# Mixture-of-experts tail on one core: the last tiles of the experts packed in halves of 64 rows, and the end of the routing rebuilt

## The chip, the cores and the metric

The kernel runs on one core of a Trainium2 chip. The metric is the device time of one execution in microseconds (us). The core has TensorE (PE in the profile; its weight loads are shown as PEld), VectorE (DVE), ScalarE (ACT), GpSimd (POOL) and SyncE (SP), each with its own instruction stream, and 16 DMA engines that all transfers share. "SPq" or "POOLq" is the sequencer of such an engine, which issues transfers and waits on semaphores. In this kernel SP issues the plain loads, and POOL issues the indirect transfers (gathers and scatters by a list of row numbers).

## The reference

The input is 4096 nodes of 512 f32 values and a dense 4096 x 4096 0/1 adjacency matrix. The program computes a masked attention with 8 heads and then a mixture of 8 experts, of which each node uses two:

```python
adj = jnp.maximum(adjacency_matrix, eye)
scores = jnp.einsum('hqk,hmk->hqm', q, k) * kd ** (-0.5)
scores = scores + IDENTITY_BIAS * eye - MASK_VAL * (1.0 - adj)
x = x + einsum('hqm,hmk,hko->qo', softmax(scores), v, Wo)      # q, k, v from layernorm(x)

logits = xf @ Wg + bg                                          # xf = layernorm(x), 8 experts
topk_scores, topk_idx = jax.lax.top_k(logits, 2)
topk_w = jax.nn.softmax(topk_scores, axis=-1)
h = gelu(einsum('nd,edh->neh', xf, W1) + b1)
y = einsum('neh,ehf->nef', h, W2) + b2
out = x + sum over the two chosen experts of topk_w * y
```

Two experts for each of 4096 nodes make 8192 rows of expert work. With the reference's inputs the eight experts get 1087, 1067, 1033, 901, 1076, 1067, 1008 and 953 rows.

## The kernel before, in words

All arithmetic is in f32, and a product of two f32 tiles is issued to TensorE as two instructions. The program has four stages.

**Projections and lists (to about 490 us).** Queries, keys and values are computed and put in DRAM, and for each tile of 128 queries a list of the keys that any of them sees is built.

**Attention (to about 1500 us).** It goes over 32 query tiles and, within each, over tiles of 128 listed keys; `items` is the list of these (query tile, key tile) pairs. POOL gathers the keys of an item `AHEAD=9` items ahead. The order of all instructions is written out by hand (`tc.manual_schedule()`): an item `n` issues the turning of keys for `n+3`, the scores of `n+2` and the value product of `n`, and between them come the jobs of `route(g)`. There, a group of finished query tiles (`GROUPS`: seven groups of four tiles, then 2, 1 and 1) is normalized, its gate logits are computed (`pg`, `pl`, `l`), the two best experts are found (`rank`, `chosen`), each row gets a place in its expert's region of `xs_d` (`place`, `slot`, `slot_i`), the running `count` per expert is raised, and the rows are scattered to `xs_d` by POOL (L825), one scatter for each query tile and each of the two choices. The scatters wait in the list `waiting`. They are issued when a group two later begins, or all at once after the last item. `slot_i` (L808, L809) has two buffers, so the third group in a row waits until the scatters of the first have read theirs.

**The end of the routing.** After the last item SP loads the second layer's weights `w2` (L1215, eight loads of 1 MB), and VectorE checks whether any sum of the attention left its safe bounds (`bad`, L1227 to L1237). The result goes to a register of every engine (L1241), and a branch skips a fallback body (L1244). Then `finish_routing` (L836 to L893) makes from `count` a table with one entry per expert tile (which expert, from which row), with operations that are 71 tiles x 8 experts wide (L860 to L877), and the marks `first` and `mine`. A tile is 128 rows of one expert's region; the last tile of an expert is laid so that it ends at the region's end, so it may overlap the one before it, and `mine` sends the overlapping rows to a spare place.

**Expert tiles (`work_off`, L1357 to L1454).** 69 tiles run (`MOSTLY`); two more stand in a branch on the register `more`, which is 0 for these inputs. For tile b:

- `fetch(b)`, four tiles ahead: SP reads expert and start row from the table (L1368, L1372) and loads 128 rows `r` (L1377, five buffers) and both biases spread over 128 partitions (`bb`, L1379 and L1380, four buffers).
- `turn` transposes the rows on TensorE (`pt_e`, L209) and ScalarE copies them (`xT`).
- `hidden` multiplies by W1 (`ph`, L1391: four f32 products of 512 columns, 8 instructions), VectorE adds b1 (L1396), ScalarE applies gelu (L1397).
- `turn_hidden` transposes that (`pht`, L1403), VectorE copies it to `hT` (L1405).
- `second` computes the gate (L1411, L1414), multiplies by W2 (`py`, L1420, 8 instructions), VectorE adds b2 (`y`, L1425, three buffers), ScalarE scales by the gate (L1426), VectorE makes the target rows `to` (L1429, L1433, eight buffers), and POOL scatters y onto the output with an add (L1434).

The scatter-adds all write the output, so each waits for the landing of the one before it:

```python
nc.gpsimd.indirect_dma_start(
    out=out,
    out_offset=bass.IndirectOffsetOnAxis(ap=to[:, 1:2].bitcast(I32), axis=0),
    in_=y, in_offset=None, compute_op=ALU.add,
)
```

In this stage a scheduler places the instructions on each engine; an engine runs its own in that order, so one that waits holds all behind it. PE's order for a tile is `pht(b)`, `ph(b+1)`, `pt_e(b+2)`, `py(b)`.

Of the kernel before, what the change touches and what calls it, by code (L numbers as in the profile page):

```python
# [20 lines left out]
P = 128  # L21
# [22 lines left out]
def kernel(  # L44
# [30 lines left out]

    nc = tc.nc
# [15 lines left out]
    NB = (2 * N + E * (P - 1)) // P  # L92
    MOSTLY = NB - 2
# [74 lines left out]
    first = const.tile([P, NB], F32, name="first")  # L168
    table = const.tile([1, 2 * NB], I32, name="table")
    mine = const.tile([P, NB], F32, name="mine")  # L170
# [621 lines left out]
    def route_3(m, l, rank, pp, rows, pool, name):  # L792
# [15 lines left out]
        slot_i = pool.tile([P, m, 2], I32, tag="slot_i", name=f"slot_i_{name}")  # L808
# [27 lines left out]
    def finish_routing(pool, psum):  # L836

        pn = psum.tile([P, E], F32, name="pn")
        nc.tensor.matmul(pn, ones, count, start=True, stop=True)
        many = pool.tile([P, E], F32, name="many")  # L840
        nc.vector.tensor_copy(many, pn)
        more = pool.tile([P, E, NT], F32, name="more")
        nc.vector.tensor_tensor(
            more, many.unsqueeze(2).to_broadcast([P, E, NT]),
            full.unsqueeze(1).to_broadcast([P, E, NT]), op=ALU.is_gt,
        )
        tiles_e = pool.tile([P, E], F32, name="tiles_e")
        nc.vector.tensor_reduce(tiles_e, more, axis=AX.X, op=ALU.add)
        none = pool.tile([P, E], F32, name="none")
        nc.vector.memset(none, 0.0)  # L850
        upto = pool.tile([P, E], F32, name="upto_e")
        nc.vector.tensor_tensor_scan(
            upto, tiles_e, none, initial=0.0, op0=ALU.add, op1=ALU.add
        )
        nc.vector.tensor_scalar(
            none[:1, :1], upto[:1, E - 1 : E], -float(MOSTLY), 0.0, op0=ALU.add, op1=ALU.max
        )
        nc.vector.tensor_copy(beyond, none[:1, :1])
        past = pool.tile([P, NB, E], F32, name="past_e")
        nc.vector.tensor_tensor(  # L860
            past, nth.unsqueeze(2).to_broadcast([P, NB, E]),
            upto.unsqueeze(1).to_broadcast([P, NB, E]), op=ALU.is_ge,
        )

        end = pool.tile([P, E + 1], F32, name="end")
        nc.vector.memset(end[:, E:], float(E * R + P))
        nc.vector.tensor_add(end[:, :E], many, start_e)
        more_e = pool.tile([P, E], F32, name="more_e")
# [33 lines left out]
    with tc.tile_pool(name="p2a", bufs=2) as two, tc.tile_pool(  # L902
# [274 lines left out]
        for n, (i, c) in enumerate(items):  # L1177
            begin()
            if n + AHEAD < len(items):
                fetch(n + AHEAD)  # L1180
            if c == 2 and i + 1 < NT:
                load_q(i + 1)
# [35 lines left out]
        while n <= len(items) + LAST or jobs or first_of_step:  # L1218
            begin()
            later(n)  # L1220
            while waiting:
                waiting.pop(0)[1]()
# [282 lines left out]
```

## Time and profile before

| | |
|---|---|
| runs | 2105.8, 2101.3, 2100.26 us (median 2101.3) |
| the profiled execution | 2098.63 us, of which its span 2096.9 us, so 1.73 us outside the span |
| mean granted TensorE clock | 0.984 |
| busy share of the span | PE 96%, PEld 64%, DVE 62%, POOL 49%, ACT 45% |
| attention's last TensorE work | about 1502 us |
| first `r` load issued | 1543.60 us |
| first `py` | 1561.21 us |
| last scatter-add begins on POOL | 2090.57 us |

The page of a profile gives the busy time of each engine, the same in 40 slices of the span, the DMA queues, the chain of waits that ended last, and the costliest groups of instructions. A line such as "1525.82 0.17 DVE L809 CAST ... [11.21 <-DMA xs_d<-rows,slot_i]" of a timeline reads: start at 1525.82 us, 0.17 us long, on VectorE, from line 809, after VectorE had been idle for 11.21 us, which a DMA that writes `xs_d` and reads `rows` and `slot_i` ended.

### The profile page before, as it was taken

To read this page: it belongs to the slowest core of one execution; us is meant where nothing else is said; L and a number is where in the kernel's file an instruction comes from. 1 tells how busy PE (TensorE), PEld (TensorE's weight loads), DVE (VectorE), ACT (ScalarE), POOL (GpSimd) and SP (SyncE) were. 2 spreads that over 40 slices of the span, in tenths; PEclk is the share of its full clock that TensorE was granted. 3 is DMA by queue.
4 is the path that set the end of the run, shared out by engine and by line. 5 is a ranking of instruction groups with operands and counts; after the bars stand their busy time and mean duration, and the time that the engine had idled before them with its cause. 6 is when DMAs were issued, how large, how long until landed. Compare 5 with 4: busy or idle time off the path is not lost. (4 is left out here: it accounts for less than half of the span.)

```text
span 2096.9 us, 48528 instructions
## 1 busy us (share of the span) xinstructions
PE 2003.1 (96%) x18748; PEld 1331.8 (64%) x18748; DVE 1290.2 (62%) x2446; ACT 941.1 (45%) x1703; POOL 1032.2 (49%) x1067
## 2 busy tenths in 40 slices
PE   8998899999999999999999999999849999999998
PEld 3444444488888788788878778777624444444443
DVE  5786778287767777777777777676733333333332
ACT  3644454365556555556556555555412222222221
POOL 1044445678776676676666657678312211222122
PEclk9999999999999999999999999999969999999999
DMA  8978898778888788788888878777666566656653
GB/s 326 369 277 291 303 316 278 213 239 257 259 272 250 244 279 255 239 276 255 269 266 249 262 213 271 231 235 239 214 186 135 135 136 139 137 133 137 137 140 77
DMA packets 213088, 479.03 MB, mean 228 GB/s; under 512 B 48963, under 2 KB 80963, under 8 KB 208757
## 3 DMA queue, kind: packets, MB, share of 16 engines
q0 software_dynamic: 78944, 241.65, 39.3%
q1 hardware_dynamic: 133380, 233.15, 36.1%
q8 instruction: 153, 2.51, 0.5%
q10 hardware_dynamic: 528, 1.05, 0.2%
q14 instruction: 83, 0.67, 0.1%
HBM read 398.85 MB, written 76.90 MB: 227 GB/s over the span
## 5 line engine op out<-in xcount | busy, mean ns | idle before, releaser
L231 POOL DMA_INDIRECT kv<-kv_d,key_of x363 | 426.0, 1174 | 241.4 <-PE po L1024 156.6
L1012 DVE TENSOR_TENSOR e<-e,mask 128x512 f32<-128x512 f32 (+1 forms) x363 | 322.8, 890 | 202.2 <-ACT e L1004 140.1
L957 ACT COPY kT<-pk 128x512 f32<-128x512 f32 x395 | 232.0, 587 | 279.5 <-PE pk L954 270.1
L1434 POOL DMA_INDIRECT out_dram<-y,to x69 | 107.7, 1561 | 450.0 <-ACT y L1426 439.2
L1030 DVE TENSOR_TENSOR acc<-acc,e 128x512 f32<-128x512 f32 (+1 forms) x363 | 321.4, 885 | 0.0
L1024 PE MATMUL po<-e,kv 128*64 128x64 f32 (+1 forms) x5808 | 303.6, 247 | 0.0
L231 POOL DMA_INDIRECT mask<-in_adjT_dram,mask_of x234 | 263.2, 1125 | 71.3 <-issue 54.2
L1024 PEld LDWEIGHTS po<-e,kv 128*64 128x64 f32 x5808 | 239.6, 137 | 43.8 <-DVE mv L198 0.2
L1001 PE MATMUL s<-q,kT 128*128 128x128 f32 x1832 | 265.1, 288 | 1.5 <-ACT acc L994 1.5
L1391 PE MATMUL ph<-w,xT 128*128 x552 | 250.6, 597 | 0.7 <-ACT xT L210 0.7
L1420 PE MATMUL py<-w,hT 128*128 x552 | 248.5, 593 | 2.0 <-DVE hT L1405 2.0
L1001 PEld LDWEIGHTS s<-q,kT 128*128 128x128 f32 x1832 | 221.6, 191 | 17.0 <-ACT acc L994 1.6
L1004 ACT ACTIVATE e<-s 128x512 f32<-128x512 f32 x229 | 137.1, 599 | 93.2 <-PE s L1001 90.9
L954 PE MATMUL pk<-ident,kv 64*128 64x64 f32 x2904 | 167.7, 235 | 11.7 <-ACT kT L957 10.9
L954 PEld LDWEIGHTS pk<-ident,kv 64*128 64x128 f32 x2904 | 118.1, 138 | 76.5 <-issue 45.9
L231 POOL DMA_INDIRECT pm<-in_adjT_dram,mask_of x129 | 125.9, 976 | 79.4 <-DMA packed_h<-pm 33.4
L1420 PEld LDWEIGHTS py<-w,hT 128*128 128x128 f32 x552 | 99.6, 190 | 102.5 <-issue 99.5
L1391 PEld LDWEIGHTS ph<-w,xT 128*128 128x128 f32 x552 | 100.2, 192 | 100.9 <-issue 99.8
L994 ACT ACTIVATE e<-s 128x512 f32<-128x512 f32 x268 | 145.6, 596 | 38.1 <-PE s L989 37.2
L989 PE MATMUL s<-q,kT 64*128 64x128 f32 x2144 | 148.8, 279 | 0.0
L373 DVE TENSOR_REDUCE flags<-adjT 128x64 f32<-128x4096 f32 x32 | 140.6, 4405 | 11.8 <-DMA adjT<-in_adjT_dram 11.8
L1426 ACT ACTIVATE y<-y,gate 128x512 f32<-128x512 f32 x69 | 49.8, 722 | 212.0 <-DVE y L1425 207.6
(611 smaller groups left out, 2582.7 us busy)
## 6 DMA issues: line engine op xcount, KB each, us to landing
adjT<-in_adjT_dram SPq DMA_DIRECT2D x32, 2048.0 KB
bb<-in_L_ffn_b_dram SPq DMA_DIRECT2D x138, 256.0 KB
r<-xs_d SPq DMA_DIRECT2D x69, 258.0 KB
kv_d<-kv SPq DMA_DIRECT2D x32, 512.0 KB
xt<-in_x_dram SPq DMA_DIRECT2D x32, 256.0 KB
qT_d<-qT SPq DMA_DIRECT2D x8, 1024.0 KB
q<-qT_d SPq DMA_DIRECT2D x64, 128.0 KB
xr<-in_x_dram SPq DMA_DIRECT2D x32, 256.0 KB
```

What stands on the lines that cost most here:

```text
L231: nc.gpsimd.indirect_dma_start(out=to, out_offset=None, in_=src, in_offset=bass.IndirectOffsetOnAxis(ap=of[:, at[i] + c : at[i] + c + 1], ...
L373: nc.vector.tensor_reduce(flags[g][:, :, j, :], adj_in.pop(i).rearrange("p c (h q) -> p h c q", h=2), axis=AX.X, op=ALU.max,)
L954: nc.tensor.transpose(pk[:, r, ts(p, KD)], kv[n][half, ts(p, P)], ident[half, half])
L957: nc.scalar.copy(kT[n].rearrange("k p (r j) -> k r p j", r=2), pk[:, :, : NP * KD].rearrange("k r (p j) -> k r p j", p=NP),)
L989: nc.tensor.matmul(s[r][:, p, :], k[rows, p, :], q_in[i][rows, p, r, :], start=True, stop=True,)
L994: nc.scalar.activation(e.rearrange("p (a r) q -> p r a q", r=2)[:, r], s[r], AF.Exp)
L1001: nc.tensor.matmul(s[:, p], k[:, p, :], q_in[i][:, p, :, q], start=True, stop=True)
L1012: nc.vector.tensor_mul(e, e, m.unsqueeze(1).to_broadcast(e.shape))
L1024: nc.tensor.matmul(po[i][r * KD : (r + 1) * KD, p, q], v[:, ts(h, KD)], e[:, h, :], start=(c < 0 and p == 0), stop=(c == listed[i] - 1), s ...
L1030: nc.vector.tensor_add(acc[i][:, :, q], acc[i][:, :, q], e)
L1391: nc.tensor.matmul(ph, xTs[b][:, c, :], w1[:, bass.ds(es[b], 1), c, :], start=(c == 0), stop=(c == DC - 1),)
L1420: nc.tensor.matmul(py, hTs[b][:, c, :], w2[:, bass.ds(es[b], 1), c, :], start=(c == 0), stop=(c == HC - 1),)
```

## The change

The expert stage now has `NF` = 57 tiles of 128 rows of one expert, as before, and then tiles of two halves of 64 rows. 57 is the least number of full tiles that any split of 8192 rows can have. What is left of the experts is cut in pieces of 64 rows: 14 whole ones at most, and per expert one last piece of under 64 rows. Tiles 57 to 64 hold one whole piece (partitions 0 to 63) and the last piece of expert h = b - 57 (partitions 64 to 127). Tile 65 holds a whole piece alone in 64 rows. So 66 tiles run; five more single pieces stand in the branch on `more`, which is 0 for these inputs too (61 full tiles of 128 can be cut from the counts, of which 57 are used, and nine whole pieces of 64 are left).

In a tile of two halves `product` issues, for each of the four chunks, one f32 product of 64 columns of the array for each half, each with its own expert's weights, so 16 instructions instead of 8 for `ph` and for `py`. `fetch` issues six loads of 64 rows instead of three of 128. `second` issues two scatter-adds: one of the first 64 rows, then one of all 128 rows in which the foreign rows (all of half 0, and what `mine` marks in half 1) are sent to the spare place. The list of targets of the second one, `to2`, has four buffers. In whole tiles `to` is now one copy.

`finish_routing` is rebuilt: it works with operations of 2 x 8 elements and puts the table together by a product with a diagonal (`all_ones`, `diag`, `pt`); it moves ahead of the check's register and branch, and a second copy of it stands in the fallback body. `slot_i` has four buffers. In the last nine items of the attention, which gather nothing any more, each step issues one waiting scatter behind a small memset. The check of the bounds moves to four steps after the last item.

```diff
-    NB = (2 * N + E * (P - 1)) // P
-    MOSTLY = NB - 2
+    HR = P // 2
+    NF = (2 * N - E * (P - 1) + P - 1) // P
+    NH = 2 * N // HR - 2 * NF
+    MOSTLY = E + 1
+    assert NH >= MOSTLY and NH <= P and NF <= P
...
+    first = const.tile([P, NF + NH], F32, name="first")
+    table = const.tile([1, 2 * (NF + NH) + E], I32, name="table")
+    mine = const.tile([P, E], F32, name="mine")
+    row_of = const.tile([P, 2], F32, name="row_of")
...
-        slot_i = pool.tile([P, m, 2], I32, tag="slot_i", name=f"slot_i_{name}")
+        slot_i = pool.tile([P, m, 2], I32, tag="slot_i", bufs=4, name=f"slot_i_{name}")
         nc.vector.tensor_copy(slot_i, slot)
...
-    def finish_routing(pool, psum):
+    def finish_routing(all_ones, pool, psum, tag, name):
+        def column(what, *width):
+            return pool.tile([P, *(width or (1,))], F32, name=f"{what}_{name}")
+        none = column("none", E)
+        nc.vector.memset(none, 0.0)
...
+        pn = psum.tile([P, E], F32, tag=tag, name=f"pn_{name}")
         nc.tensor.matmul(pn, ones, count, start=True, stop=True)
+        ints = pool.tile([P, E], I32, name=f"ints_{name}")
+        nc.vector.tensor_copy(ints, pn)
+        nc.vector.tensor_single_scalar(ints, ints, 7, op=ALU.arith_shift_right)
+        nc.vector.tensor_copy(tiles[:, 0], ints)
         nc.vector.tensor_tensor_scan(
+            upto[:, 0], tiles[:, 0], none, initial=0.0, op0=ALU.add, op1=ALU.add
+        )
+        nc.vector.tensor_sub(used[:, :E], upto[:, 0], tiles[:, 0])
         nc.vector.tensor_scalar(
+            used[:, :E], used[:, :E], -1.0, float(NF), op0=ALU.mult, op1=ALU.add
+        )
+        nc.vector.scalar_tensor_tensor(
+            used[:, :E], used[:, :E], 0.0, tiles[:, 0], op0=ALU.max, op1=ALU.min
+        )
+        rest = column("rest", E)
+        nc.vector.scalar_tensor_tensor(
+            rest, used[:, :E], -float(P), pn, op0=ALU.mult, op1=ALU.add
+        )
+        nc.vector.tensor_copy(ints, rest)
+        nc.vector.tensor_single_scalar(ints, ints, 6, op=ALU.arith_shift_right)
+        nc.vector.tensor_copy(tiles[:, 1], ints)
+        nc.vector.tensor_tensor_scan(
+            upto[:, 1], tiles[:, 1], none, initial=0.0, op0=ALU.add, op1=ALU.add
+        )
+        nc.vector.tensor_scalar(
+            per_e[:, 0], tiles[:, 0], -float(P), float(R), op0=ALU.mult, op1=ALU.add
+        )
+        nc.vector.tensor_sub(per_e[:, 1], used[:, 1:], used[:, :E])
+        nc.vector.scalar_tensor_tensor(
+            per_e[:, 1], per_e[:, 1], 2.0, tiles[:, 1], op0=ALU.mult, op1=ALU.subtract
+        )
+        nc.vector.tensor_scalar(
+            per_e[:, 1], per_e[:, 1], float(HR), float(R), op0=ALU.mult, op1=ALU.add
+        )
+        past = column("past", 2, E)
+        nc.vector.tensor_scalar(past, upto, number, None, op0=ALU.is_le)
+        nc.vector.tensor_mul(per_e, per_e, past)
+        of = column("of", 2, 2)
+        sums = column("sums", 2)
+        nc.vector.tensor_reduce(sums, per_e, axis=AX.X, op=ALU.add)
+        nc.vector.tensor_reduce(of[:, :, 0], past, axis=AX.X, op=ALU.add)
+        nc.vector.tensor_scalar_min(of[:, :, 0], of[:, :, 0], float(E - 1))
+        nc.vector.tensor_add(of[:, :, 1], sums, row_of)
...
+        diag = column("diag", 2 * (NF + NH))
+        for k, (at_k, n) in enumerate(((0, NF), (2 * NF, NH))):
+            nc.vector.tensor_mul(
+                diag[:, at_k : at_k + 2 * n].rearrange("p (j b) -> p j b", j=2),
+                ident[:, :n].unsqueeze(1).to_broadcast([P, 2, n]),
+                of[:, k].unsqueeze(2).to_broadcast([P, 2, n]),
+            )
+        pt = psum.tile([P, 2 * (NF + NH)], F32, tag=tag, name=f"pt_{name}")
+        nc.tensor.matmul(pt, all_ones, diag, start=True, stop=True)
+        nc.vector.tensor_add(end, pn, start_e)
+        nc.vector.tensor_scalar_add(table[:, 2 * (NF + NH) :], end[:1], -float(HR))
+        nc.vector.tensor_copy(table[:, : 2 * (NF + NH)], pt[:1])
+        nc.vector.tensor_scalar(first[:, :NF], pt[:, NF : 2 * NF], number, None, op0=ALU.add)
+        nc.vector.tensor_scalar(
+            first[:HR, NF:], pt[:HR, 2 * NF + NH :], number[:HR], None, op0=ALU.add
+        )
+        nc.vector.tensor_scalar(
+            first[HR:, NF : NF + E], end[HR:], number[HR:], -float(P),
+            op0=ALU.add, op1=ALU.add,
+        )
+        nc.vector.scalar_tensor_tensor(
+            rest, tiles[:, 1], -float(HR), rest, op0=ALU.mult, op1=ALU.add
+        )
+        nc.vector.tensor_scalar(mine, rest, from_end, None, op0=ALU.is_ge)
+        nc.vector.tensor_scalar(
+            none[:1, :1], upto[:1, 1, E - 1 : E], -float(MOSTLY), 0.0,
+            op0=ALU.add, op1=ALU.max,
         )
         nc.vector.tensor_copy(beyond, none[:1, :1])
...
+        between = fixed.tile([P, 1], F32, name="between")
...
             if n + AHEAD < len(items):
                 fetch(n + AHEAD)
+            elif waiting:
+                nc.gpsimd.memset(between, 0.0)
+                waiting.pop(0)[1]()
...
-        nth = endp.tile([P, NB], F32, name="nth")
-        nc.gpsimd.iota(nth, pattern=[[1, NB]], base=0, channel_multiplier=0,
-                       allow_small_or_imprecise_dtypes=True)
+        all_ones = endp.tile([P, P], F32, name="all_ones")
+        nc.gpsimd.memset(all_ones, 1.0)
         for e in range(E):
             nc.sync.dma_start(out=w2[:, e], in_=W2[e].rearrange("(c p) f -> p c f", p=P))
         order.__exit__(None, None, None)
+        def check_all():
+            bad = small.tile([P, NT, 5], F32, name="bad")
...
+            nc.vector.tensor_copy(redo, pf[:1])
         n = len(items)
         while n <= len(items) + LAST or jobs or first_of_step:
             begin()
             later(n)
+            if n == len(items) + 4:
+                check_all()
             while waiting:
                 waiting.pop(0)[1]()
             n += 1
...
+        finish_routing(all_ones, endp, ps_e, "e", "")
...
+        with tc.tile_pool(name="g4", bufs=1) as one, tc.tile_pool(
+            name="g4p", bufs=1, space=PSUM
+        ) as psum:
+            finish_routing(all_ones, one, psum, "n", "g")
     end_cm.__exit__(None, None, None)
...
             def fetch(b):
+                r = work.tile([P, W], F32, tag="row", bufs=5, name=f"r_{b}")
+                bb = work.tile([P, 2, D], F32, tag="bb", bufs=4, name=f"bb_{b}")
+                h = b - NF
+                n = P if h < 0 else HR
+                e_at, f_at = (b, NF + b) if h < 0 else (2 * NF + h, 2 * NF + NH + h)
                 e = nc.values_load(
-                    table[:, b : b + 1], engines=(SP, PE), min_val=0, max_val=E - 1,
+                    table[:, e_at : e_at + 1], engines=(SP, PE), min_val=0, max_val=E - 1,
                     skip_runtime_bounds_check_because=why,
                 )
...
-                rows[b], es[b], bs[b] = r, e, bb
+                parts[b] = [(slice(0, n), bass.ds(e, 1), f_at)]
+                if 0 <= h < E:
+                    parts[b].append((slice(HR, P), slice(h, h + 1), 2 * (NF + NH) + h))
+                for of, ex, at_f in parts[b]:
+                    f = nc.values_load(
+                        table[:, at_f : at_f + 1], engines=(SP,), min_val=0, max_val=E * R,
+                        skip_runtime_bounds_check_because=why,
+                    )
+                    nc.sync.dma_start(out=r[of], in_=xs_d[bass.ds(f, n), :])
+                    for k, src in enumerate((b1, b2)):
+                        nc.sync.dma_start(
+                            out=bb[of, k], in_=src[ex, :].partition_broadcast(n)
+                        )
+                rows[b], bs[b] = r, bb
+            def product(to, b, xT, w, chunks):
+                for c in range(chunks):
+                    for of, ex, _ in parts[b]:
+                        nc.tensor.matmul(
+                            to[of], xT[:, c, of], w[:, ex, c, :],
+                            start=(c == 0), stop=(c == chunks - 1), skip_group_check=True,
+                        )
+            def size(b):
+                return P if b < NF + E else HR
...
             def hidden(b):
                 ph = ps_h.tile([P, HID], F32, tag="h", name=f"ph_{b}")
-                for c in range(DC):
-                    nc.tensor.matmul(
-                        ph, xTs[b][:, c, :], w1[:, bass.ds(es[b], 1), c, :],
-                        start=(c == 0), stop=(c == DC - 1),
-                    )
+                m = size(b)
+                product(ph, b, xTs[b], w1, DC)
...
             def second(b):
-                r = rows[b]
+                r, m = rows[b], size(b)
...
                 py = ps_y.tile([P, D], F32, tag="y", name=f"py_{b}")
-                for c in range(HC):
-                    nc.tensor.matmul(
-                        py, hTs[b][:, c, :], w2[:, bass.ds(es[b], 1), c, :],
-                        start=(c == 0), stop=(c == HC - 1),
+                product(py, b, hTs[b], w2, HC)
+                y = work.tile([P, D], F32, tag="y", bufs=3, name=f"y_{b}")
+                nc.vector.tensor_add(y[:m], py[:m], bs[b][:m, 1])
+                nc.scalar.mul(y[:m], y[:m], gate[:m, 1:2])
+                own = P if b < NF else HR
+                to = work.tile([P, 1], I32, tag="to", bufs=8, name=f"to_{b}")
+                nc.vector.tensor_copy(to[:own], r[:own, D : D + 1].bitcast(I32))
+                all_to = [(own, to)]
+                if m > own:
+                    less = work.tile([P, 1], F32, tag="less", name=f"less_{b}")
+                    to = work.tile([P, 1], I32, tag="to2", bufs=4, name=f"to2_{b}")
+                    h = b - NF
+                    nc.vector.scalar_tensor_tensor(
+                        less, r[:, D : D + 1].bitcast(I32), spare, mine[:, h : h + 1],
+                        op0=ALU.subtract, op1=ALU.mult,
                     )
-                y = work.tile([P, D], F32, tag="y", bufs=3, name=f"y_{b}")
-                nc.vector.tensor_add(y, py, bs[b][:, 1])
-                nc.scalar.mul(y, y, gate[:, 1:2])
...
+                    nc.vector.tensor_add(to, less, spare)
+                    all_to.append((P, to))
+                for n, to in all_to:
+                    nc.gpsimd.indirect_dma_start(
+                        out=out, out_offset=bass.IndirectOffsetOnAxis(ap=to[:n, 0:1], axis=0),
+                        in_=y[:n], in_offset=None, compute_op=ALU.add,
+                    )
...
-    work_off(0, MOSTLY, "")
+    work_off(0, NF + MOSTLY, "")
     with tc.If(more > 0):
-        work_off(MOSTLY, NB, "m")
+        work_off(NF + MOSTLY, NF + NH, "m")
```

## Prediction

> **What bounds the kernel now.** I read the page first, then the busy time by stretches around the end of the attention, then the chain of waits over the last 600 us, and for the places where it leaves TensorE the timelines of VectorE, POOL and SP. The page gives the span, and its last slices show that the chip is not short of transfers in the expert stage.
>
> ```profile
> span 2096.9 us, 48528 instructions
> ...
> PEclk9999999999999999999999999999969999999999
> DMA  8978898778888788788888878777666566656653
> ```
>
> The stretches of 1500 to 1546 us and 1561 to 2000 us (core time, busy us of each engine, granted clock, DMA share, GB/s):
>
> ```profile
> 1500.00:1546.00 46.00, 12.01 (x102) 7.24 (x101) 23.27 (x120) 6.10 (x17) 12.17 (x13) 0.63 0.74 267
> 1561.00:2000.00 439.00, 438.79 (x1359) 216.55 (x1360) 156.19 (x398) 104.15 (x170) 87.43 (x56) 1.00 0.61 135
> ```
>
> So there are two regimes. In the expert tiles TensorE is busy for 438.79 of 439 us: TensorE bounds them. Before them there is a hole in which it works for 12 of 46 us. VectorE's timeline shows what the hole is made of: first a wait of 11.21 us for a scatter to let go of a `slot_i` buffer, then 3.97 us, then the wide operations until the table stands.
>
> ```profile
> 1525.82 0.17 DVE L809 CAST slot_i<-slot 128x2 int32<-128x2 f32 x1 [11.21 <-DMA xs_d<-rows,slot_i]
> ...
> 1528.88 0.14 DVE L1237 CAST redo<-pf 1x1 int32<-1x1 f32 x1
> ...
> 1535.32 0.17 DVE L841 COPY many<-pn 128x8 f32<-128x8 f32 x1 [3.97 <-PE pn L839]
> ...
> 1542.31 0.18 DVE L890 CAST table<-begin 1x71 int32<-1x71 f32 x1
> ```
>
> SP's waits say the same from the side of the loads (waited for, us in total, times, longest): it waits for the check, for its own branch, for the table.
>
> ```profile
> SPq L1372 <- DVE begin L891: 8.6, 1, 8.6
> ...
> SPq L1244 <- SPq L1244: 3.8, 1, 3.8
> ```
>
> At the end of the program the chain (start, duration, what) goes over TensorE with one pair of products after the other and leaves it for the scatter-adds:
>
> ```profile
> 2076.52 3.44 PE ph L1391 x8
> 2079.95 3.45 PE py L1420 x8
> ...
> 2085.15 4.67 DMA out_dram<-y,to
> 2089.82 0.02 issue
> 2089.84 0.02 POOLq L1434
> 2089.86 0.50 issue
> 2090.36 0.31 POOLq L1456
> 2090.67 1.46 POOL out_dram L1434
> ```
>
> To be seen there: a scatter takes 4.67 us to land, and the next one starts 5.4 us after it (2085.15, 2090.57), with nothing else in transfer. POOL's timeline amid loads shows more:
>
> ```profile
> 1707.16 1.56 POOL L1434 DMA_INDIRECT out_dram<-y,to  x1 [7.26 <-ACT y L1426]
> 1714.41 1.56 POOL L1434 DMA_INDIRECT out_dram<-y,to  x1 [5.69 <-ACT y L1426]
> 1721.81 1.56 POOL L1434 DMA_INDIRECT out_dram<-y,to  x1 [5.84 <-ACT y L1426]
> ```
>
> After a late one they come 7.25 and 7.40 us apart, closer than TensorE's 7.745 us per tile. The page names ScalarE, but y was long ready: that is the chain of landings, catching up. It has 0.4 us to spare per tile today.
>
> **Part 1, the hole.** The sum is for SP's first `r` load (1543.60 before). With four buffers for `slot_i` the wait of 11.21 us is gone; next late is the last group's `pl`, which TensorE had finished at 1518.28. From l to `count` took 1.84 us (1526.60 to 1528.44), so `count` stands at 1520.2. The new `finish_routing` has some 33 small VectorE operations up to the table, at 0.2 us each as in VectorE's rows 1526.33 to 1526.53, and two trips to TensorE, 0.5 us: 1527.5 instead of 1542.5. SP then reads the check's register (0.6) and goes through its branch (3.8): 1531.9. The last `xs_d` scatters and the 8 MB of `w2` are the competing ends: DMA runs at about 395 GB/s until some 1531, so the loads can go out at 1531 to 1532.2. I take 1531.9, a gain of **11.7 us**. Bounds: 14.5 if the branch runs before the table, 9 if all the late ends add up. The longer fallback body in the skipped branch is priced at 0 by the branch's own row; if skipping grows with the body, it is up to 3.8 more. From the first load to the first `py` it was 17.6 us, set by the first twelve loads (one `r` takes 9.14 us); these are the same. The moved check (eight operations) lies where VectorE was idle, else 1.6 us; the nine memsets and early scatters are hidden by a POOL that is busy for 51 of the last 80 us of the attention, else 9 x 1.3 us.
>
> **Part 2, the tiles on TensorE.** 57 whole tiles stay at 7.745 us (3.44 + 3.44 + 2 x 0.43); one copy less on VectorE has no waiter. Before, twelve more followed: 92.9 us. Do two column halves run at once? The nearest rows are in the attention:
>
> ```profile
> 1476.52 1.16 PE L1001 MATMUL s<-q,kT 128*128 128x128 f32 x8
> 1477.61 1.09 PE L1024 MATMUL po<-acc,kv_-1_18809 128*64 128x128 f32 x16
> ```
>
> Sixteen instructions of 64 columns take what eight of 128 take. So sixteen of 512 elements cost 3.44 us, too. Steps between forms of a tile are about 0.2 us there instead of 0.1; at four per tile 0.6 (0 to 1.2): 8.35 us. The single half has nothing beside it and costs 7.7. TensorE alone: 8 x 8.35 + 7.7 = 74.5, 18.4 us less than before. If the halves do not overlap, 8 x 15.2 + 7.7 = 129.3, 36 more.
>
> **Part 3, the scatters.** Each two-half tile issues two scatter-adds on the output, and in the built program the second waits for the first's landing and the next tile's for the second's. Packet records show the rows of an unloaded scatter written from 2.1 to 4.4 us after its start, of a loaded one from 3.9 to 6.3; the semaphore follows after 0.33, the next start after 0.8 more. Half the rows halve only the writing. First scatter to next start: 4.4 us unloaded, 6.3 loaded (bounds 3.6 and 7.4). Second: 5.5 (2085.15 to 2090.67 in the chain; bounds 5.2 and 7.4). The pair needs 9.9 to 11.8 us while TensorE needs 8.35: the scatter chain becomes the bound.
>
> It also holds TensorE. On VectorE, `to2` of tile 61 stands ahead of `y` of tile 58 and waits, with four buffers, for the second scatter of tile 57; the same for 62, 63 and 64 ahead of y(59), y(60) and y(61). Behind it on VectorE wait y, the next `hT` and the next b1 add, and so PE. For these four tiles the period is: to2, to and wake 0.5, y to POOL 1.72 (2006.41 to 2008.13 for tile 57), first scatter 6.3 amid six loads, second 4.67 to its landing: 13.2; unloaded 11.3. I take **12.7**, nearer the loaded row, as the loads of tiles 62 to 65 fall into it.
>
> Whole section from y(57) to the span's end: before 90.5 (2006.41 to 2096.9). After: 0.6 for switches, 4 x 12.7, then 1.72 to POOL, four pairs at 9.9 with nothing left to load, and the last scatter of 64 rows to the end 5.2 (before 6.33 with 128). Sum 0.6 + 50.8 + 1.7 + 39.6 + 5.2 = 97.9: a **loss of 7.4 us**, bounds 2.6 less than before (P 11.3, pairs 8.8) to 20.6 more (P 15, pairs 10.9). The six loads per tile cost SP about 6 x 0.55 and three register reads of 0.27, 4.1 us, inside the period.
>
> A page of the Trainium skill, "DMA: Bandwidth & Descriptors", section "Anatomy of one DMA", puts a GpSimd transfer at a fixed 2.0 us plus bytes at 436 GB/s, most of the fixed part being the wait for the write's receipt. It speaks against a split into two, as the fixed part is paid twice, but 256 KB would be 2.6 us, where this trace shows 4.67. By the page a pair with its wakes would be about 6.6 us, below TensorE's 8.35, and the packing would pay in full; the measured row decides, so I do not take it.
>
> **Sum.** 2096.9 - 11.7 + 7.4 = 2092.6 of span, 2094.3 with the 1.73 outside. The median of the runs is 2.7 above the profiled execution: **2097.0 us** on the median's scale, 0.2% below 2101.3. About 0.3%, 6.3 us, is what a measurement here can tell from no change.
>
> **Rivals.**
> - *The packing pays.* Were the scatters no bound, the packing saves 18.4 + 1.1 and the time is 2101.3 - 11.7 - 19.5 = 2070. For it: DMA share of only 0.61 in the stage. Against it: even one unloaded 128-row scatter needs 5.4 us and the second waits for it. With all lower bounds the chain gives 2101.3 - 11.7 - 2.6 = 2087. Chance 0.12, with times of 2070 to 2088.
> - *The scatters cost more, and it gets slower.* Place: period of tiles 58 to 61 and the pairs after. If the second scatter, too, is slowed by loads (7.4 instead of 5.5), P is 15 and the loss is 7.4 + 4 x 2.3 = 16.6: 2106; with pairs of 10.9 it is 20.6: 2110. From P = 13.8 the whole change is a loss, from P = 15.4 by over 0.3%. For it: xs_d scatters at 1481 to 1519 us, beside heavy loads, were 7.1 us apart (1512.12, 1519.22). Chance 0.23, times 2102 to 2116.
> - *The halves do not overlap.* 36 - 1 - 11.7: 2125. The po row speaks against it. Chance 0.05.
> - *The hole stays long*, as the branch, `xs_d` or `w2` end late: gain 5 instead of 11.7, 2103.7. For it: three ends lie within 2 us. Chance 0.05.
> - That the extra halves in the branch run would add five tiles; the counts of rows exclude it.
>
> **How the numbers follow.** The forecast has 0.55 and its own range 2088 to 2106; about 0.22 of it lies below 2095.0, 0.31 between, 0.02 above 2107.6. Faster: 0.22 + 0.12 = 0.34. Same: 0.31 + 0.07 of the second rival + 0.05 = 0.43. Slower: 0.02 + 0.16 + 0.05 = 0.23. The range 2086 to 2112 leaves out half of the first rival, the top of the second and the third.
>
> **What would show it.** Right: VectorE's `slot_i` without a long wait, first `r` load near 1532, py of tile 57 in 16 instructions of about 3.5 us, POOL with two scatters per tile about 6 and 5.5 us apart, VectorE idle for 3 to 5 us before each `to2` with the scatter named, TensorE out of work after tile 62. Wrong: pairs of scatters under 8.4 us, a py of 6.9 us, or a first load after 1536.

## The result, and the profile after

The changed kernel takes 2104.47 us (median of 4 runs, 2102.64 to 2106.95), the kernel before beside it 2100.78 us. The ratio is 1.0014, with a 95% interval of 0.9993 to 1.0035. A second, longer comparison (12 runs) gave 0.9999 (0.9989 to 1.0009). The change makes no difference that can be measured. The forecast was 2097 us, 0.2% faster, in a range of 2086 to 2112. Of its two large terms, the loss at the end came out near its size, though by two errors that cancel; the gain in the hole was taken some 40% too large, for a reason that the runs show.

The page of the kernel after, in the lines shown of before:

```profile
span 2105.3 us, 48550 instructions
...
PEclk9999899999999999999999999999979999999998
DMA  8978998678888788788887878778675665555543
```

The stretches of the kernel after (core time, busy us of PE, PEld, DVE, ACT and POOL, granted clock, DMA share, GB/s): the hole, the whole tiles, and the tiles of two halves with the tail.

```profile
1508.00:1546.00 38.00, 13.01 (x110) 7.74 (x104) 19.41 (x131) 6.39 (x17) 8.02 (x9) 0.67 0.83 297
1565.00:1980.00 415.00, 415.00 (x1287) 204.61 (x1286) 135.65 (x323) 98.51 (x162) 83.86 (x54) 1.00 0.60 136
2008.00:2105.00 97.00, 62.99 (x270) 21.47 (x266) 19.49 (x51) 13.62 (x22) 25.30 (x17) 0.88 0.39 70
```

The whole tiles are as before, TensorE is always busy. In the last 97 us it works for 63. There, the chain that ended last no longer has TensorE in it at all; it goes from scatter to scatter (start, duration, what):

```profile
2084.16 4.88 DMA out_dram<-y,to
...
2089.79 3.69 DMA out_dram<-y,to
...
2094.23 4.68 DMA out_dram<-y,to
...
2099.45 0.31 POOLq L1548
2099.76 1.32 POOL out_dram L1527
```

VectorE's waits between 1975 and 2060 us (waited for, us in total, times, longest) show the lock by `to2`, and a wait that had not been foreseen: the copy of the targets of a later tile, which stands ahead of y, waits for that tile's rows.

```profile
DVE to L1524 <- DMA out_dram<-y,to: 22.8, 4, 6.0
...
DVE to L1512 <- DMA r<-xs_d: 11.2, 4, 3.3
```

Both stand ahead of y (L1508) in VectorE's timeline, the copy ahead of y of tile 57 and the lock ahead of y of tile 58:

```profile
2007.97 0.14 DVE L1512 COPY to<-r 64x1 int32<-64x1 int32 x1 [2.67 <-DMA r<-xs_d]
2008.06 0.69 DVE L1508 TENSOR_TENSOR y<-py,bb 128x512 f32<-128x512 f32 x1
...
2019.60 0.16 DVE L1524 TENSOR_TENSOR to<-less,spare 128x1 int32<-128x1 f32 x1 [5.98 <-DMA out_dram<-y,to]
2019.68 0.14 DVE L1512 COPY to<-r 64x1 int32<-64x1 int32 x1
2019.74 0.69 DVE L1508 TENSOR_TENSOR y<-py,bb 128x512 f32<-128x512 f32 x1
```

To compare runs, the time is cut at four events: the start of the last output product of the attention (**A**: L1071 before, L1126 after; at 1505.04 us before, so TensorE's last work there is later than the 1502 us of the table of before), SP's first load of expert rows (**r0**), the start of VectorE's y of tile 57 (**y57**), the end of the span. All in us, from one profiled execution each:

| kernel | A | A to r0 | r0 to y57 | y57 to end | span |
|---|---|---|---|---|---|
| before | 1505.0 | 38.6 | 462.8 | 90.5 | 2096.9 |
| after | 1513.3 | 30.0 | 464.8 | 97.2 | 2105.3 |

The routing part gains 8.6 us, the tiles up to 57 lose 2.0, the section behind them 6.7: together 0.1. What is left of the difference, 8.3 us, came before A, in the projections and the attention. The first experiment is on that.

### The profile page after: what moved, and what is told of

Its sections match the earlier page's. It is cut to its first block, busy times and chain, and to the rows that moved or that the text cites. A ratio compares the mean times of both kernels' runs of the same rounds, so it can differ in the third digit from the quotient of the medians.

```text
span 2105.3 us, 48550 instructions
## 1 busy us (share of the span) xinstructions
PE 1994.6 (95%) x18806; PEld 1318.0 (63%) x18806; DVE 1265.9 (60%) x2385; ACT 934.4 (44%) x1694; POOL 1033.9 (49%) x1081
## 5 line engine op out<-in xcount | busy, mean ns | idle before, releaser
L247 POOL DMA_INDIRECT kv<-kv_d,key_of x363 | 431.9, 1190 | 251.5 <-PE po L1079 169.7
L1527 POOL DMA_INDIRECT out_dram<-y,to x74 | 113.8, 1538 | 453.6 <-ACT y L1509 401.6
L247 POOL DMA_INDIRECT mask<-in_adjT_dram,mask_of x234 | 255.6, 1092 | 71.3 <-issue 54.9
L1460 PE MATMUL py<-w,hT 128*128 (+1 forms) x592 | 242.3, 607 | 11.8 <-DVE hT L1492 11.7
L1460 PE MATMUL ph<-w,xT 128*128 (+1 forms) x592 | 240.2, 598 | 0.7 <-ACT xT L1474 0.7
L1009 PE MATMUL pk<-ident,kv 64*128 64x64 f32 x2904 | 168.3, 235 | 11.8 <-ACT kT L1012 10.9
L1460 PEld LDWEIGHTS py<-w,hT 128*128 128x128 f32 (+1 forms) x592 | 92.9, 180 | 114.3 <-issue 100.6
L1460 PEld LDWEIGHTS ph<-w,xT 128*128 128x128 f32 (+1 forms) x592 | 92.4, 179 | 100.5 <-issue 99.4
```

The costliest lines, as they stand in the source:

```text
L247: nc.gpsimd.indirect_dma_start(out=to, out_offset=None, in_=src, in_offset=bass.IndirectOffsetOnAxis(ap=of[:, at[i] + c : at[i] + c + 1], ...
L1009: nc.tensor.transpose(pk[:, r, ts(p, KD)], kv[n][half, ts(p, P)], ident[half, half])
L1460: nc.tensor.matmul(to[of], xT[:, c, of], w[:, ex, c, :], start=(c == 0), stop=(c == chunks - 1), skip_group_check=True,)
```

## The experiments

The rows of the table above for all kernels that were run:

| kernel | A | A to r0 | r0 to y57 | y57 to end | span | ratio to before (95%) |
|---|---|---|---|---|---|---|
| before_again | 1510.7 | 38.0 | 462.9 | 89.6 | 2101.1 | one run |
| after_again | 1511.0 | 30.0 | 464.6 | 96.2 | 2101.7 | 0.9999 (0.9989 to 1.0009) |
| hole_alone | 1510.8 | 30.3 | 465.0 | 90.7 | 2096.8 | 0.9963 (0.9951 to 0.9974) |
| pack_alone | 1512.8 | 36.1 | 465.8 | 97.8 | 2112.4 | 1.0029 (1.0017 to 1.0040) |
| to2_8 | 1511.6 | 30.4 | 465.1 | 94.2 | 2101.3 | 0.9986 (0.9976 to 0.9996) |
| second_only | 1510.0 | 30.1 | 465.5 | 72.0 | 2077.6 | 0.9891 (0.9872 to 0.9911) |
| w2_half | 1514.2 | 29.6 | 464.3 | 96.0 | 2104.1 | 1.0015 (1.0005 to 1.0025) |
| no_w2 | 1509.0 | 26.6 | 466.3 | 96.4 | 2098.4 | 0.9995 (0.9983 to 1.0007) |

### Whose are the 8 us before A?

> The kernel before once more, unchanged, for the part of the time that belongs to no line of the change. In the two profiles at hand the last product of the attention starts at 1505.04 us before and at 1513.32 us after, although up to there the change adds only a few small operations. Theory A (it is the execution, not the change): in this profile that product starts some us away from 1505, anywhere from 1502 to 1514. Theory B (it belongs to the change): it starts at 1505 within 1 us.

> The changed kernel once more, unchanged, timed in five rounds. From the profiles at hand, three stretches can be told apart: from the last product of the attention to the first load of expert rows 38.6 us before and 30.0 after; from there to y of tile 57 462.8 and 464.8; from there to the end of the span 90.5 and 97.2. The sum of these is the same within 0.1 us. Theory A: the time is that of before within 2 us, ratio 0.999 to 1.001, and the last product of the attention starts at another time than 1513. Theory B: ratio 1.003 to 1.004, with that product at 1513 within 1 us.

The kernel before, run again, reaches A 5.7 us later than in its first profile, and the kernel after 2.4 us earlier than in its own. A line of each timeline, of the first profile of before, of `before_again`, and of the first profile of after:

```profile
1505.04 3.70 PE L1071 MATMUL py<-wo,o 128*128 128x512 f32 x8 [0.67 <-DVE o L1066]
```

```profile
1510.70 3.70 PE L1071 MATMUL py<-wo,o 128*128 128x512 f32 x8 [0.67 <-DVE o L1066]
```

```profile
1513.32 3.70 PE L1126 MATMUL py<-wo,o 128*128 128x512 f32 x8 [0.67 <-DVE o L1121]
```

So A scatters by several us from execution to execution with the same program, and theory A holds: 1510.7 and 1511.0 for the two kernels when run again. In the first two profiles 5.6 of the 8.3 us had arisen by 447 us, in the projections and lists, and the rest in one step near 700 us; behind it, every item of the attention was late by the same amount. Single profiles of this kernel can't be compared by their spans to better than some 8 us, but the stretches behind A can.

### The two parts, one at a time

`hole_alone` is the kernel before with the routing part (the old `finish_routing`, its tiles given names, moved):

```diff
-        slot_i = pool.tile([P, m, 2], I32, tag="slot_i", name=f"slot_i_{name}")
+        slot_i = pool.tile([P, m, 2], I32, tag="slot_i", bufs=4, name=f"slot_i_{name}")
...
+            elif waiting:
+                nc.gpsimd.memset(between, 0.0)
+                waiting.pop(0)[1]()
...
+            if n == len(items) + 4:
+                check_all()
...
+        finish_routing(nth, endp, ps_e, "e", "")
     first_scatters = list(scatters)
     again = nc.values_load(
...
-    with tc.tile_pool(name="ps_end", bufs=1, space=PSUM) as psum:
-        finish_routing(endp, psum)
```

> The kernel before with only the routing part of the change: four buffers for slot_i, one waiting scatter in each of the last nine items behind a memset, the check four steps after the last item, and the end of the routing ahead of the check's register and branch (the old wide operations, 69 whole tiles; a copy in the fallback body). My theory: the first load of expert rows waits for the landing of w2, not for the table, so the old wide operations cost nothing: 30 to 31 us from the last product of the attention to that load instead of 38.6, and about 2092.5 us in all, ratio 0.996. Rival (the table bounds, and the new small operations are what pays): 33 to 35 us, 2096 us.

30.3 us and a ratio of 0.9963: 7.8 us of 2104 are gained by this part alone, without any of the new operations. The last entries of the table of `hole_alone` are written from 1534.11 on, 23.3 us behind A (with the new operations in `after`: 1534.91, 21.6 behind A), and the first load comes only 0.3 us later than in `after`. A table that is ready 1.7 us earlier is worth almost nothing; what bounds instead is shown below (the floor of the hole).

`pack_alone` is the kernel after with these edits undone:

```diff
-        slot_i = pool.tile([P, m, 2], I32, tag="slot_i", bufs=4, name=f"slot_i_{name}")
+        slot_i = pool.tile([P, m, 2], I32, tag="slot_i", name=f"slot_i_{name}")
...
-            elif waiting:
-                nc.gpsimd.memset(between, 0.0)
-                waiting.pop(0)[1]()
...
-        finish_routing(all_ones, endp, ps_e, "e", "")
+        check_all()
...
+    with tc.tile_pool(name="ps_end", bufs=1, space=PSUM) as psum:
+        finish_routing(all_ones, endp, psum, "n", "")
```

> The changed kernel with the routing part undone: slot_i with two buffers, no scatters in the last items, the check and the end of the routing (the new one) in their old places. If the two parts add up: 38 us from the last product of the attention to the first load (the new end of the routing takes 5 us instead of 7 behind the branch, so 36 to 38), 97 us from y of tile 57 to the end, about 2107 to 2109 us, ratio 1.003 to 1.004. Rival (the packing costs nothing by itself, the later start of the tiles was the matter): 90 us at the end and 2101 us.

36.1 us to the first load, 97.8 at the end, ratio 1.0029, by that 6.1 us more than before: the packing by itself makes the kernel slower. The two parts add up, 0.9963 and 1.0029 to 0.9992, where both together were measured at 0.9999, within the intervals.

### What the packing runs into

`to2_8` takes the lock away: more buffers, so that VectorE has no landing to wait for.

```diff
-                    to = work.tile([P, 1], I32, tag="to2", bufs=4, name=f"to2_{b}")
+                    to = work.tile([P, 1], I32, tag="to2", bufs=8, name=f"to2_{b}")
```

> The changed kernel with eight buffers for to2 instead of four, so that VectorE needs no landing of a scatter ahead of y of tiles 58 to 61. The pairs of scatters still wait for each other. Theory (lock and chain both cost): tiles 58 to 61 come no longer 11.7 to 12.3 us apart but at the pace of the scatter chain, 9.9 to 10.7, with y up to three buffers ahead; from y of tile 57 to the end 91 to 94 us instead of 97.2, so 3 to 6 us less. Rival (the lock is all of the loss): 78 us, 19 less. Rival (the lock costs nothing, the chain alone sets the pace): 97.

94.2 us instead of the 96.2 to 97.2 of the changed kernel, just short of the gain that was expected. The lock costs 2 to 3 us of its own; the rest is the chain of landings. The chain was slower than expected: the pairs of tiles 57 to 61 begin 10.8 to 11.8 us apart there, where 9.9 to 10.7 had been taken, hardly faster than the 11.7 to 12.3 with the lock. POOL's timeline of `to2_8`, from the second scatter of tile 63 on:

```profile
2080.24 1.56 POOL L1527 DMA_INDIRECT out_dram<-y,to  x1 [3.02 <-DMA out_dram<-y,to]
2085.88 1.42 POOL L1527 DMA_INDIRECT out_dram<-y,to  x1 [4.08 <-DMA out_dram<-y,to]
2090.21 1.56 POOL L1527 DMA_INDIRECT out_dram<-y,to  x1 [2.91 <-DMA out_dram<-y,to]
2095.63 1.42 POOL L1527 DMA_INDIRECT out_dram<-y,to  x1 [3.86 <-DMA out_dram<-y,to]
```

In this last stretch the scatter of 64 rows (1.42 us on POOL) holds up the next one for 4.3 us, that of 128 rows (1.56) for 5.4 to 5.6: half the rows take four fifths of the time.

`second_only` issues only the second scatter of a tile of two halves, so the sums of half 0 of tiles 57 to 64 are left out of the output:

```diff
-                    all_to.append((P, to))
+                    all_to = [(P, to)]
```

> The changed kernel with only the second scatter of a tile of two halves (128 rows, half 0 sent to the spare place); the sums of half 0 of tiles 57 to 64 are left out of the output. One scatter per tile, as in a whole tile. Theory (the second scatter per tile is what eats the packing): TensorE bounds again, tiles at 8.35 us, from y of tile 57 to the end 71 to 75 us instead of 97.2. Rival (what slows these tiles is the six loads or the products of 64 columns): 85 to 95 us.

72.0 us, 24 less than with both. With one scatter per tile TensorE bounds again; 16 products of 64 columns, six loads and all else are still there. So behind y of tile 57 it is the second scatter per tile, and not the products or the loads, that eats the packing. A stretch of `second_only` (columns as above):

```profile
2005.00:2065.00 60.00, 59.00 (x270) 20.69 (x266) 19.04 (x50) 13.09 (x21) 12.43 (x8) 1.00 0.43 90
```

### The floor of the hole

> The changed kernel with only the first four of the eight experts' second-layer weights loaded; the other four are set to zero by POOL, so the output of experts 4 to 7 is left out. Theory (the first load of expert rows waits until the eight loads of w2 and the last store of the attention have landed, some 10 us behind the table's 1534.91): 25 to 26 us from the last product of the attention to that load instead of 30.0, set then by SP's branch or by the last scatters to xs_d, 4 to 5 us less in all. Rival (SP's branch sets it): 30 us, no gain.

```diff
-        for e in range(E):
+        nc.gpsimd.memset(w2[:, E // 2 :], 0.0)
+        for e in range(E // 2):
             nc.sync.dma_start(out=w2[:, e], in_=W2[e].rearrange("(c p) f -> p c f", p=P))
```

The first load came 29.6 us behind A, so by that distance the theory had fallen. But the experiment disturbed itself: during POOL's memset of 6.93 us two small operations of VectorE that else take 0.20 us each (`bad`, L1279 and L1280) took 5.17 and 4.77, TensorE stood idle for 5.24 us, and the product at A then took 6.65 us instead of 3.70, which alone puts 2.95 us into the distance. Read from the table instead of from A, the first load came after 4.9 us (1538.93 to 1543.81) instead of 8.4 (1534.91 to 1543.30 in `after`). So w2 has a part, and something else is close behind it. `no_w2` shows both without a stand-in: it does not load w2, and the second product uses W1, so the output is another.

```diff
-        for e in range(E):
-            nc.sync.dma_start(out=w2[:, e], in_=W2[e].rearrange("(c p) f -> p c f", p=P))
...
-                product(py, b, hTs[b], w2, HC)
+                product(py, b, hTs[b], w1, HC)
```

> The changed kernel without the loads of w2: the second product of every expert tile uses W1, so the output is not the reference's. In the run with half of w2 the distance from the table to the first load of expert rows fell from 8.4 us to 4.9, but the memset that stood in for the other half held VectorE for 5 us and hid it in the total. Here nothing stands in. Theory (two ends lie close together: the landing of w2, and VectorE's own way through the branch behind the table, on which SP's read of the table waits): the last product of the attention to the first load 26 to 27 us instead of 30.0, set by VectorE's branch of about 3 us. Rival (w2 is all of it): the first load follows the table within 2 us, 23.5 us. Rival (w2 has no part): 30 us.

26.6 us, as expected. SP's waits around the branch (waited for, us in total, times, longest), first of `after`:

```profile
SPq L1307 <- SPq L1307: 12.3, 4, 5.9
```

and of `no_w2`:

```profile
SPq L1443 <- DVEq L1305: 16.7, 1, 16.7
...
SPq L1305 <- SPq L1305: 2.7, 1, 2.7
```

In `after`, SP needs 5.9 us for the jump at its branch (L1307), and then waits there three times more for transfers to land, the last at 1541.2 to 1541.9: that is w2 and the last store of the attention. Only then does it read the table, though that has stood since 1534.91. Without w2 the jump takes 2.7 us and nothing has to land; now SP waits for VectorE's sequencer at its own branch (L1305), which VectorE reaches only behind the table and passes in 3.0 us (1531.45 to 1534.46 in the trace). In `after` VectorE's own way through the branch is longer, 5.6 us, from the start of its branch instruction to that of the semaphore instruction behind it (duration in ns, then first and last start in us):

```profile
L1307 DVEq COMPARE_BRANCH  x1: 72/72/72, 1535.5 to 1535.5; - x1
...
L1307 DVEq EVENT_SEMAPHORE  x1: 21/21/21, 1541.2 to 1541.2; - x1
```

So with w2 two ends lie together, VectorE's at 1541.2 and SP's last landing at 1541.9, and without w2 both come earlier. The passages were longer in the runs where the DMA engines were busier meanwhile: VectorE's took 3.0 us at a DMA share of 0.03 (`no_w2`), 4.3 at 0.51 (`hole_alone`) and 5.6 at 0.81 (`after`). Why is not shown. In the total `no_w2` did not gain that (0.9995 with an interval of 0.9983 to 1.0007), which these few runs can't resolve.

### A version that beats both

`interleaved` is the changed kernel with its 66 tiles in another order: a tile of two halves behind every seven whole ones.

```diff
+    EVERY = (NF - 1) // E
...
-            for b in range(from_b, to_b):
-                if b + 4 < to_b:
-                    fetch(b + 4)
+            for n, b in enumerate(todo):
+                if n + 4 < len(todo):
+                    fetch(todo[n + 4])
                 turn_hidden(b)
...
-    work_off(0, NF + MOSTLY, "")
+    todo = list(range(NF))
+    for h in range(E):
+        todo.insert(EVERY * (h + 1) + h, NF + h)
+    work_off(todo + [NF + E], "")
```

> The changed kernel with the same 66 tiles in another order: after every seven whole tiles one tile of two halves, then the last whole tile and the single half. Nothing else is changed. The chain of scatters has about 0.4 us to spare at every whole tile, and a pair needs about 2 us more than the 8.35 us of its tile. Theory: with three buffers for y the delay of a pair is taken up by the seven whole tiles behind it, and TensorE bounds nearly throughout: 57 x 7.745 + 8 x 8.4 + 7.7 = 516 us from the first y to the last instead of 524 before; with the tail, 17 us less than the changed kernel, about 2085 us, ratio 0.992. Rival (each pair stops TensorE by 3 us wherever it stands): 24 us lost, no gain over 2100.

2078.4 us (median of 4 runs, 2076.95 to 2080.09), ratio 0.9879 (0.9860 to 0.9898): 25 us less than before, where 17 less than the changed kernel, which equals before, had been expected. From r0 to the end it takes 536.3 us, where the changed kernel takes 560.7 and the kernel before 552.4 (run again). From 1561 to 2060 us every microsecond is TensorE's:

```profile
1561.00:2060.00 499.00, 499.00 (x1655) 235.73 (x1654) 160.44 (x397) 117.40 (x191) 109.92 (x72) 1.00 0.63 133
```

POOL's timeline there shows a pair (1.45 us on POOL for 64 rows, then 128) and how the delay is made good in the tiles behind it:

```profile
1617.66 1.45 POOL L1528 DMA_INDIRECT out_dram<-y,to  x1 [5.87 <-ACT y L1510]
1624.10 1.56 POOL L1528 DMA_INDIRECT out_dram<-y,to  x1 [4.99 <-DVE y L1509]
1632.58 1.56 POOL L1528 DMA_INDIRECT out_dram<-y,to  x1 [6.92 <-DMA out_dram<-y,to]
1640.90 1.56 POOL L1528 DMA_INDIRECT out_dram<-y,to  x1 [6.75 <-DMA out_dram<-y,to]
1648.98 1.56 POOL L1528 DMA_INDIRECT out_dram<-y,to  x1 [6.53 <-DMA out_dram<-y,to]
1655.40 1.56 POOL L1528 DMA_INDIRECT out_dram<-y,to  x1 [4.85 <-DMA out_dram<-y,to]
1661.00 1.55 POOL L1528 DMA_INDIRECT out_dram<-y,to  x1 [4.04 <-ACT h L1484]
1666.71 1.55 POOL L1528 DMA_INDIRECT out_dram<-y,to  x1 [4.15 <-ACT y L1510]
```

After the pair the scatters lag, then come 5.6 and 5.7 us apart, closer than TensorE's 7.745, while TensorE's busy time shows no gap. The chain's slack is thus larger than the 0.4 us per whole tile that the prediction read from one late stretch: 7.745 less 5.6 is up to 2.1 us. The lock by `to2` does not arise in this order either, as VectorE has no wait for a landing through it. The 25 us are the whole saving on TensorE (19.5 in the prediction's rival "the packing pays") and the 7.8 us of the hole, less some 2; the expectation had counted too much of it as lost again.

## Why the prediction was right or wrong, point by point

- **Which regime bounds what.** Right. TensorE bounds the whole tiles (415 of 415 us), the hole has its own ends.
- **The hole, 11.7 us.** Too much: 8.0 to 8.6 us (38.6 and 38.0 to 30.0). The term up to the table was right, even a little careful: forecast 22.5 us behind A (1527.5), measured 21.6. What failed is the step behind it, "SP then reads the check's register (0.6) and goes through its branch (3.8): 1531.9", and that DMA is loaded "until some 1531", 26.0 us behind A. SP's branch did not lie behind the table (SP came to it at 1529.5, 5.4 us earlier); SP sat in it until w2 and the last store had landed, 27.9 and 28.6 us behind A. And VectorE's passage through the same branch, 3.0 to 5.6 us behind the table, had not been priced at all, though the profile of before has it:

```profile
L1244 DVEq COMPARE_BRANCH  x1: 72/72/72, 1531.8 to 1531.8; - x1
...
L1244 DVEq EVENT_SEMAPHORE  x1: 21/21/21, 1534.9 to 1534.9; - x1
```

  These 3.1 us are most of the 3.97 us before `many` that the prediction shows as a wait for PE. The gain stayed below even the low bound of 9 us, "if all the late ends add up", by 0.4 to 1 us. That the branch's price moves with the loads beside it (SP 2.7 without w2 and 5.9 with) makes a price from one row a poor one.
- **The tiles on TensorE.** Right. The halves overlap: sixteen instructions of 64 columns take as long as eight of 128. From TensorE's timeline of `after`:

```profile
1985.99 3.60 PE L1460 MATMUL py<-w,hT 128*128 x8
...
2002.17 3.65 PE L1460 MATMUL py<-w,hT 128*64 x16
```

  In a run of two-half tiles py to py is 8.35 us where nothing waits (2002.17 to 2010.52): exactly what was taken. The 0.6 us in it for changes of form is in part luck, as four changes at 0.1 us more, the prediction's own terms, make 0.4. The Trainium skill's page "TensorEngine Tiling (Array Packing)", section "Theoretical Speedup", says up to 2x for a dimension of 64 or less; 3.65 us against 3.60 shows it reached here.
- **Tiles 54 to 57.** The prediction had no loss ahead of y(57), and 0.6 us for changes of form behind it. From y(53) to y(57), the packed orders without interleaving take 2.1 to 3.9 us more than four whole tiles, 8.1 to 9.2 us from y to y in `after`, and `hole_alone` with whole tiles takes none more (`before_again` 1.1). TensorE lost only 0.7 of it (py(53) to py(57) in 31.67 us, four whole tiles 30.98); y(57) began 2.2 us after its product was done, and with it the chain of scatters. The list `to` of the tile four ahead stands ahead of y on VectorE and waits for that tile's rows. SP issues these rows behind the four bias loads of the tile before, and the bias loads wait for a `bb` buffer that the y before frees (VectorE's y of tile 56, then SP's timeline):

```profile
1999.92 0.69 DVE L1508 TENSOR_TENSOR y<-py,bb 128x512 f32<-128x512 f32 x1
...
2000.64 1.16 SPq L1451 DMA_DIRECT2D bb<-in_L_ffn_b_dram  x2
2002.30 0.47 SPq L1449 DMA_DIRECT2D r<-xs_d  x1
2002.82 1.23 SPq L1451 DMA_DIRECT2D bb<-in_L_ffn_b_dram  x2
2005.33 0.49 SPq L1449 DMA_DIRECT2D r<-xs_d  x1
```

  The last of these lands just before the copy at 2007.97 and y of tile 57 at 2008.06. So y waits for y through SP's queue; I had costed the six loads by SP's time alone. The stretch from r0 to y57 as a whole is a weaker sign: `hole_alone` is 2.2 us longer there than before, too, without late tiles at its end.
- **The section from y(57), a loss of 7.4.** Measured 6.7. The mechanism is the one that was described, but that the size fits is luck: two terms were off against each other, by 3.4 us too much and 2.9 too little. The period of tiles 58 to 61, taken as 12.7, is 11.7, 11.8, 11.7 and 12.3 (the first scatters start at 2009.78, 2021.46, 2033.24, 2044.92 and 2057.19): nearer the unloaded row than the loaded, as the first scatter held the second for 4.9 to 5.2 us amid the loads instead of 6.3. The pairs behind them, taken as 9.9, are 10.5, 11.3, 10.8 and 9.9. Only the last is as forecast; in the three before it the 64-row scatter held the next for 5.0 to 5.7 us instead of 4.4, and why stays open:

```profile
2057.19 1.42 POOL L1527 DMA_INDIRECT out_dram<-y,to  x1 [5.52 <-ACT y L1509]
2062.18 1.57 POOL L1527 DMA_INDIRECT out_dram<-y,to  x1 [3.57 <-DMA out_dram<-y,to]
2067.72 1.42 POOL L1527 DMA_INDIRECT out_dram<-y,to  x1 [3.97 <-ACT xT L1474]
2073.39 1.56 POOL L1527 DMA_INDIRECT out_dram<-y,to  x1 [4.25 <-issue]
```

- **The rule of the skill that was weighed.** The page "DMA: Bandwidth & Descriptors", section "Anatomy of one DMA", would have had 2.3 and 2.6 us for the two scatters, an estimate from its fixed part and rate. The chain of `after` shows 3.69 us and 4.68 to 4.88. That most of the cost is fixed, and so paid twice, agrees (half the bytes save 0.99 of 4.68 us); the size does not. By the page's size the packing would have paid in full.
- **The sum.** Forecast -4.3 us; by stretches -8.3, +1.8 and +6.7, so +0.2 (means of both profiles of each kernel), and the longer comparison has -0.1 (2103.81 to 2103.92). "Same" was the likeliest of the three cases, at 0.43.

## What to carry to other kernels

A chain of dependent transfers is a resource with a rate: before an edit puts a second link per tile on it, compare the time of the pair with the bound engine's time per tile, and look for where the slack lies. The same eight expensive tiles that cost 7 us in a row at the end cost TensorE nothing when spread among whole tiles, where the chain has slack to catch up and the buffers of `to2` come free in time. And when a table is made earlier, every engine's way from it to its first use has to be walked through: a branch is passed by each engine for itself, and SP waited there for transfers that have nothing to do with the branch.

## What the runs showed of the hardware that I had not expected

- Halving a scatter-add from 128 to 64 rows shortens its landing from 4.68 to 3.69 us at the end of `after`, and POOL's own part only from 1.56 to 1.42.
- The way of an engine through a branch that is not taken took SP 2.7 us in `no_w2`, at a DMA share of 0.38 in that time, and 5.9 in `after`, at a full one beside the 8 MB of w2; VectorE 3.0 (share 0.03) and 5.6 (0.81).
- While POOL's memset of 128 x 8192 elements ran (6.93 us, `w2_half`), two VectorE operations of 0.20 us took about 5; they ended 0.1 us after it.
- After an idle time of 3.4 or 3.9 us TensorE's next product took 5.35 us instead of 3.65, while after 2.16 us it did not (2021.09, 2032.87 and 2056.82 in `after`). Behind the scatters this cost nothing here:

```profile
2021.09 3.65 PE L1460 MATMUL py<-w,hT 128*64 x16 [2.16 <-DVE hT L1492]
...
2032.87 5.35 PE L1460 MATMUL py<-w,hT 128*64 x16 [3.37 <-DVE hT L1492]
```

- The part before A varied from 1505.0 to 1513.3 us between profiles of kernels that do the same work there.
